# A two-layer graph network on one core: another order for the first loads, another division of the output loop

## The chip, the cores and the metric

The kernel runs on one core of one Trainium2 chip. The metric is the device time of one execution in microseconds. Three runs were made of the kernel before: the median is 2925.94 us.

## The reference, cut to what matters

There are 16 graphs of 1024 nodes with 128 features. `adj` is symmetric in its pattern, not in its values, and about 6% full.

```python
# layer 0: three convolutions on the full adj
h = relu(layernorm(x))
for i in range(3):
    h = h @ W[i] + b[i]
    nh = h / norm(h)                      # per node
    h = (adj * (nh @ nh.T)) @ h           # relu after it, except the last
x = x + h
# layer 1
h = relu(layernorm(x))
adj_d = dilate(adj, mask)                 # rows one after the other drop neighbours, their columns too
h1 = bn(relu(sage(h,  adj_d, Wr1, Wx1, ...)))
h2 = bn(relu(sage(h1, adj_d, Wr2, Wx2, ...)))
h3 = bn(relu(sage(h2, adj_d, Wr3, Wx3, ...)))
return x + (concat(h1, h2, h3) * mf @ Wl + bl) * mf      # mf: the mask as floats
```

`bn` takes its means over all batches and nodes, so nothing of h3's projection can start before the last batch has been through the last `sage`.

## The kernel before, in words

All matrices are float32 and are cut into blocks of 128 x 128; a batch has 8 x 8 of them. The program has four parts.

The **fused first stage** (to about 1720 us) is layer 0 and the dilation together. Both are Python generators. `step0` advances layer 0 by one step, and the loop over `dilation()` advances layer 0 in proportion to estimated costs, so that the two are woven into one program. What an engine then executes is not this order itself: a scheduler sets each engine's instructions in a static order of its own, from priorities and the dependences between tiles. Inside one engine's queue an instruction waits for all that stand before it.

In layer 0 the adjacency of a batch is kept as transposed blocks of one triangle beside the plain blocks of the other. For each block row `q`, taken in the order `SEQ = (0, 7, 1, 6, 2, 5, 3, 4)`, `adj_piece` (L223) loads the block column `nat` through SP's queue (one of two buffers), and `adjT_tile` (L229) loads the plain row (L233), transposes the 8 - q blocks of `nat` on TensorE (L240), copies them out of PSUM on ScalarE into `adjA` (L241) and writes them to DRAM by GpSimd's queue (L242). `adjA` has two places, for an even and an odd batch.

A `Batch` has these steps: `fetch` loads x (L253); `norm` is layer norm and relu, with bn_stats on VectorE (L140) and eight activations on ScalarE (L148); `enter` transposes it to `hT` (L165, L166); `features` multiplies by W (L273) and adds b on VectorE (L277); `turned` makes `nhT`, `scaled` takes the row norms on ScalarE (L299) and makes `hS` on GpSimd (L301). Then for each `q` follow `products` (TensorE L324, VectorE L333 and L336 into `ew`), `turn` (L353, L354), `sums` and `sums_back` (L364, L378).

`layer0` (L419) begins with all eight `adjT_tile` of batch 0, with `enter` and `features` placed among them, then `turned` and `scaled`. Only then come the products. The other batches' pieces are listed in `pieces` with the place (which batch's turn in `order`, which of its eight steps) at which they are to be transposed: batch 1's during the first turn, each later batch's two turns ahead.

Ahead of this the program writes its constants: W and b through ScalarE's queue (L180, L181), the triangular constants `upto`, `off`, `after` from two fills `up` on GpSimd (L188, L190), and the mask: `mi` is loaded through ScalarE's queue (L202), cast on VectorE (L204), transposed on TensorE (L206) and turned into `mf` and `mbias` (L208, L212). `mbias` is first read in the dilation (L586), `mf2 = mf * mf` (L757) in the output loop. The first calls are x of batch 0, two `adj_piece`, `norm`, x of batch 1, and then layer 0's first step (L737 to L742).

In the dilation, each row of adj is loaded by SP (`an`, L545), turned into 0 and 1 on ScalarE (L547, L548), solved by rounds of small matmuls, and scanned on VectorE (L699).

The **first `sage`** (about 1740 to 2180 us) applies the dilated pattern to adj, and the **second and third `sage`** (to about 2870 us) read the result back from DRAM.

The **output loop** (L1067 to L1075) is last. For each batch, `normed` (L1004) makes `hT` with one activation of 128 x 1024 (L1006, two buffers), `project` (L1011) makes two halves of four matmuls into PSUM (L1016, three buffers, shared), and eight VectorE operations (L1072) compute y = pp * mf2 + acc. SP then writes y to `out` (L1075). y lies in pool tag "o", which has two buffers.

Of the kernel before, what the change touches and what calls it, by code (L numbers as in the profile page):

```python
# [8 lines left out]
F32 = mybir.dt.float32  # L9
F16 = mybir.dt.float16  # L10
I32 = mybir.dt.int32
AF = mybir.ActivationFunctionType
ALU = mybir.AluOpType
# [33 lines left out]
def tile_adj_preln_d2(  # L47
# [121 lines left out]
    with ExitStack() as actx:  # L169
# [7 lines left out]
        w0 = pool1.tile([P, 3, P], F32, name="w0")  # L177
        b0 = pool1.tile([P, 3, P], F32, name="b0")
        for i in range(3):
            nc.scalar.dma_start(w0[:, i, :], W[i])  # L180
            nc.scalar.dma_start(b0[:, i, :], bW[i].partition_broadcast(P))  # L181

        upto = pool1.tile([P, P], F16, name="upto")
        off = pool1.tile([P, P], F16, name="off")
        after = pool1.tile([P, P], F16, name="after")
        for fill, value, op in ((0.0, -2.0, ALU.is_ge), (4.0 * FAR, 2.0 * FAR, ALU.is_gt)):
            up = pool2.tile([P, NCH, P], F32, tag="tt", name=f"up_{fill}")[:, 0, :]
            nc.gpsimd.memset(up, value)  # L188

            nc.gpsimd.affine_select(  # L190
                up, up, pattern=[[1, P]], compare_op=op, fill=fill, base=0, channel_multiplier=-1
            )
            if fill:
                nc.vector.tensor_copy(after, up)
            else:
                nc.vector.scalar_tensor_tensor(upto, ident, 2.0 - FAR, up, ALU.mult, ALU.add)
        nc.vector.tensor_scalar(off, ident, -FAR, None, ALU.mult)
        one16 = pool1.tile([P, 1], F16, name="one16")
        nc.vector.memset(one16, 1.0)

        mi = pool2.tile([P, NCH, P], I32, tag="xb", name="mi")[:NB, 0, :]
        nc.scalar.dma_start(mi, nodemask.rearrange("b (c p) -> (b c) p", p=P))  # L202
        mfl = pool2.tile([P, NCH, P], F32, tag="tt", name="mfl")[:NB, 0, :]
        nc.vector.tensor_copy(mfl, mi)  # L204
        mt = ps_sm.tile([P, NB], F32, tag="sm", name="mt")
        nc.tensor.transpose(mt, mfl, ident[:NB, :NB])  # L206
        mf_flat = mf.rearrange("p b c -> p (b c)")
        nc.vector.tensor_copy(mf_flat, mt)  # L208

        mbias = pool1.tile([P, B, NCH], F32, name="mbias")  # L210
        mb_flat = mbias.rearrange("p b c -> p (b c)")
        nc.vector.tensor_scalar(mb_flat, mf_flat, 0.0, NEVER, ALU.is_equal, ALU.mult)  # L212

# [205 lines left out]
        def layer0():  # L419

            pieces = [((0, s), (1, SEQ[s])) for s in range(NCH)]
            for b in range(2, B):
                i = 6 * (b // 2) - 2 + b % 2
                for s in range(NCH):
                    at_ = min(2 * s + 2 - b % 2, 2 * NCH - 1)
                    pieces.append(((i + at_ // NCH, at_ % NCH), (b, SEQ[s])))
            pieces.sort()  # L430
            for s in range(NCH):
                adjT_tile(0, SEQ[s])
                if s < NCH - 2:
                    adj_piece(0, SEQ[s + 2])
                if s == 3:
                    order[0].enter(0)
                    order[0].enter(1)
                if 4 <= s < 4 + NHALF:
                    order[0].features(s - 4)
            order[0].turned()  # L440
            order[0].scaled()
            for (_, _), piece in pieces[:2]:
                adj_piece(*piece)
            yield 0.0
            behind, pieces_at = [], 0
            for i, now in enumerate(order + [None]):
                then = order[i + 1] if i + 1 < len(order) else None
                after = order[i + 2] if i + 2 < len(order) else None
                ended = order[i - 1] if i and order[i - 1] is not then else None
                if now:  # L450
                    now.begin()
                for s in range(NCH if now else LAG):
                    q = SEQ[s]
                    if now:
                        behind.append((now, s, *now.products(s)))
                        yield (NCH - q) * COLS
                    late = None
# [12 lines left out]
                    if not now:  # L470
                        continue
                    while pieces_at < len(pieces) and pieces[pieces_at][0] == (i, s):
                        adjT_tile(*pieces[pieces_at][1])
                        pieces_at += 1
                        if pieces_at + 1 < len(pieces):
                            adj_piece(*pieces[pieces_at + 1][1])
                        yield (NCH - pieces[pieces_at - 1][1][1]) * TURN
                    if ended:
                        if s == 1:
                            ended.fetch()  # L480
                        if s == 3:
                            ended.residual()
                            yield NCH * TURN
                        if s == 5:
                            ended.next_layer()
                    if s == 5 and after and first(i + 2):
                        after.fetch()
                    if then:
                        new = first(i + 1)
                        if s == 0 and new:  # L490
                            then.norm()
                        if s == 3 and new:
                            then.enter(0)
                            then.enter(1)
                            yield NCH * TURN
                        if s == 4 or s == 5:
                            then.features(s - 4)
                            yield CPH * COLS
                        if s == 6:
                            then.turned()  # L500
                            then.scaled()
                            yield NCH * TURN
# [232 lines left out]
            return got is not None  # L735

        batches[0].fetch()  # L737
        adj_piece(0, SEQ[0])
        adj_piece(0, SEQ[1])
        batches[0].norm()  # L740
        batches[1].fetch()
        step0()  # L742
        for weight in dilation():
            done += weight
            while at * total < done * SPREAD * total0 and step0():
# [29 lines left out]
    with ExitStack() as bctx:  # L775
# [289 lines left out]
            ab = batchnorm(l)  # L1065

        for b in range(B):  # L1067
            y = pool2.tile([P, NCH, D], F32, tag="o", name=f"y_{b}")
            for h, pp, a in project(2, b, normed(3, b, ab)):
                for c in range(CPH):  # L1070
                    n = h * CPH + c
                    nc.vector.scalar_tensor_tensor(  # L1072
# [53 lines left out]
```

## Time and profile before

| what | value |
|---|---|
| median of three runs | 2925.94 us (2923.68 to 2931.75) |
| the profiled execution, whole | 2932.24 us |
| its span, first to last instruction | 2930.4 us |
| granted TensorE clock, mean | 0.976 |
| busy: TensorE, VectorE, ScalarE, GpSimd | 2673.3, 1955.9, 1420.2, 452.9 us |
| first transposes of adj (L240) | 17.9 us |
| first products (L324) | 45.63 us |
| first and last y operation (L1072) | 2879.7 and 2925.3 us |

The span is shorter than the time by 1.8 us that lie around it. Times inside the span count from its first instruction. An engine's busy time is a sum over the whole program; which resource decides changes from stage to stage, so stages are read by themselves: busy time by stretch, then who waited for whom, then the chain that is followed back from the last instruction.

### The profile page before, as it was taken

How to read it: one execution, taken by the hardware profiler on the slowest of the kernel's cores; microseconds unless marked ns; L12 is line 12 of the kernel's file. 1: busy time of each engine (PE TensorE's matmuls, PEld its weight loads, DVE VectorE, ACT ScalarE, POOL GpSimd, SP SyncE). 2: the span in 40 equal slices, each digit the busy share in tenths (PEclk: the TensorE clock that was granted, in tenths of full speed). 3: DMA queues.
4: the chain of work that ended last, by engine and by line, in shares of the span. 5: the costliest groups of instructions: out<-in, count | busy, mean ns of one | idle time of the engine just before them, and what ended most of it. 6: DMA issues, size and time to landing. Idle time of an engine off the chain costs nothing.

```text
span 2930.4 us, 51972 instructions
## 1 busy us (share of the span) xinstructions
PE 2673.3 (91%) x18803; PEld 2205.6 (75%) x18803; DVE 1955.9 (67%) x4945; ACT 1420.2 (48%) x4069; POOL 452.9 (15%) x604
## 2 busy tenths in 40 slices
PE   5898998998989989998998979999989999899996
PEld 3666666666666666766666758989979999899996
DVE  2777778877977878788778446777772233455555
ACT  5766667557546546455455323333333333333333
POOL 2111112012011112121112002222220010010010
PEclk9999999999999999999999989999999999999998
DMA  8437258247347456386162039999995666576763
GB/s 268 145 115 219 89 168 247 77 139 229 92 130 219 105 169 188 95 248 176 39 206 105 1 114 403 405 406 404 405 372 173 208 210 202 177 243 222 240 217 115
DMA packets 383017, 585.21 MB, mean 200 GB/s; under 512 B 85201, under 2 KB 267345, under 8 KB 382753
## 3 DMA queue, kind: packets, MB, share of 16 engines
q1 hardware_dynamic: 343280, 425.28, 45.9%
q0 software_dynamic: 38464, 156.07, 14.4%
q8 instruction: 151, 2.47, 0.3%
q14 instruction: 114, 0.93, 0.1%
q10 hardware_dynamic: 1008, 0.46, 0.1%
HBM read 403.44 MB, written 163.58 MB: 193 GB/s over the span
## 4 chain that ended last, share of the span: by engine, by line
PE 56%; DVE 18%; DMA 13%; issue 6%; ACT 4%; POOL 1%; SPq 1%; POOLq 0%; DVEq 0%; another core or an unknown queue 0%; ACTq 0%
PE agg L831 20%; PE po L364 7%; PE pg L324 6%; DVE rank L699 5%; PE pw L803 5%; PE po L378 5%; DVE ew L336 4%; DMA aT<-in_adj_dram 3%; PE gt L353 3%; PE pp L1016 2%; DMA kl<-keep 2%; PE pw L273 2%; DMA an<-in_adj_dram 2%; DMA aT<-adjT 1%; DMA kb<-keep 1%
## 5 line engine op out<-in xcount | busy, mean ns | idle before, releaser
L831 PE MATMUL agg<-hw,aT 128*128 128x128 f32 (+1 forms) x6144 | 742.9, 277 | 8.8 <-DVE aT L941 7.5
L831 PEld LDWEIGHTS agg<-hw,aT 128*128 128x128 f32 x6144 | 712.1, 192 | 14.7 <-DVE aT L941 10.1
L324 PE MATMUL pg<-nhT 128*128 128x512 f32 (+3 forms) x1152 | 457.4, 500 | 71.9 <-DVE ew L336 63.0
L364 PE MATMUL po<-ew,hS 128*128 128x512 f32 (+3 forms) x1152 | 455.3, 499 | 13.8 <-ACT hTo L387 9.9
L336 DVE TENSOR_TENSOR ew<-pg,adjA 128x768 f32<-128x768 f32 (+3 forms) x528 | 425.1, 827 | 4.6 <-DVEq L768 2.7
L378 PE MATMUL po<-ew,hS 128*128 128x128 f32 x2688 | 366.9, 277 | 0.0
L378 PEld LDWEIGHTS po<-ew,hS 128*128 128x128 f32 x2688 | 339.3, 193 | 36.6 <-issue 36.3
L354 ACT ACTIVATE ew<-gt 128x512 f32<-128x512 f32 (+1 forms) x480 | 208.9, 465 | 243.2 <-PE gt L353 240.2
L324 PEld LDWEIGHTS pg<-nhT 128*128 128x128 f32 x1152 | 188.7, 193 | 171.6 <-issue 120.9
L699 DVE TENSOR_TENSOR_SCAN rank<-patt 128x1024 f16<-128x1024 f16 x128 | 294.0, 2307 | 0.9
L364 PEld LDWEIGHTS po<-ew,hS 128*128 128x128 f32 x1152 | 195.8, 194 | 105.6 <-issue 72.9
L353 PEld LDWEIGHTS gt<-ident,ew 128*128 128x128 f32 x1344 | 167.8, 143 | 97.3 <-issue 68.5
L333 DVE TENSOR_TENSOR ew<-pg,adjA 128x128 f32<-128x128 f32 x384 | 108.1, 282 | 196.3 <-PE pg L324 150.9
L353 PE MATMUL gt<-ident,ew 128*128 128x128 f32 x1344 | 212.1, 277 | 4.1 <-ACT ew L354 2.7
L881 POOL TENSOR_TENSOR o<-o,rn 128x512 f32<-128x512 f32 x96 | 107.6, 1121 | 650.4 <-DVE rn L880 646.0
L803 PE MATMUL pw<-wrx,hT 128*128 128x256 f32 x768 | 181.1, 391 | 10.2 <-ACT hT L1006 9.7
L805 DVE TENSOR_TENSOR own<-pw,bs 128x256 f32<-128x256 f32 x192 | 81.4, 424 | 148.0 <-ACT hw L804 148.0
L803 PEld LDWEIGHTS pw<-wrx,hT 128*128 128x128 f32 x768 | 146.3, 196 | 32.7 <-ACT hT L1006 10.5
L959 ACT ACTIVATE aT<-pta 128x512 f32<-128x512 f32 (+3 forms) x160 | 71.2, 466 | 205.0 <-PE pta L958 178.0
L860 DVE SCALAR_TENSOR_TENSOR o<-agg,invdeg,own 128x128 f32<-128x128 f32 x384 | 109.7, 344 | 87.0 <-PE agg L831 78.3
L876 ACT ACTIVATE own<-o 128x128 f32<-128x128 f32 x384 | 114.6, 301 | 103.3 <-DVE o L860 103.2
L301 POOL TENSOR_TENSOR hS<-hN,rn 128x1024 f32<-128x1024 f32 x48 | 94.6, 1970 | 409.2 <-DVE rn L157 300.4
(161 smaller groups left out, 3962.2 us busy)
## 6 DMA issues: line engine op xcount, KB each, us to landing
an<-in_adj_dram SPq DMA_DIRECT2D x128, 512.0 KB, 4.6
keep<-kp POOLq DMA_DIRECT2D x128, 256.0 KB, 3.6
kb<-keep SPq DMA_DIRECT2D x128, 256.0 KB, 5.4
aT<-adT SPq DMA_DIRECT2D x32, 960.0 KB, 5.4
aT<-adT SPq DMA_DIRECT2D x32, 832.0 KB, 5.5
aT<-adT SPq DMA_DIRECT2D x32, 704.0 KB, 4.6
aT<-adT SPq DMA_DIRECT2D x32, 576.0 KB, 3.4
xb<-in_x_dram SPq DMA_DIRECT2D x31, 512.0 KB, 5.1
```

The lines of the kernel that those rows point to most:

```text
L324: nc.tensor.matmul(pg[:, :n, :].rearrange("p c q -> p (c q)"), lhsT=self.nhT[:, q * P : (q + 1) * P], rhs=self.nhT[:, (q + c) * P : (q + c ...
L333: nc.vector.tensor_tensor(ew[:, 0, :], pg[:, 0, :], place[:, 0, :], ALU.mult)
L336: nc.vector.tensor_tensor(both[0][:, :, off, :], pg[:, own:n, :].unsqueeze(1).to_broadcast([P, 2, n - own, P]), both[1][:, :, off, :], ALU ...
L353: nc.tensor.transpose(pt[:, i, :], ew[:, at + i, :], ident)
L354: nc.scalar.activation(ew[:, at : at + n, :], pt[:, :n, :], AF.Copy)
L364: nc.tensor.matmul(self.po[:, c * P : (c + n) * P], lhsT=self.hS[:, q, :], rhs=ew[:, c - q : c - q + n, :].rearrange("p c q -> p (c q)"), ...
L378: nc.tensor.matmul(self.po[:, q * P : (q + 1) * P], lhsT=self.hS[:, q + n, :], rhs=ew[:, NCH - 1 - q + n, :], start=False, stop=closes and ...
L699: nc.vector.tensor_tensor_scan(rank, pt[:, 1 : N + 1], pt[:, 2:], 0.0, ALU.add, ALU.add)
L803: nc.tensor.matmul(pw[:, i, :], lhsT=hT[:, 2 * h + i, :], rhs=wrx[:, l, :], start=True, stop=True)
L831: nc.tensor.matmul(self.place(c), lhsT=aT[:, blk, :], rhs=self.hw[:, source, :], start=source == 0 and c % self.ga == 0, stop=ends(c, source),
L860: nc.vector.scalar_tensor_tensor(self.o[:, c, :], self.place(c)[:, :P], invdeg[:, b, c : c + 1], self.own[:, c, :], ALU.mult, ALU.add,)
L876: nc.scalar.activation(self.own[:, n, :], self.o[:, n, :], AF.Square, accum_out=ss[:, c : c + 1])
```

## The change

At the start, x of batch 0 is requested ahead of adj; W, b and the mask are issued on GpSimd's queue; the mask's work comes after layer 0's first step; the two fills `up` and the mask get small tiles of their own, in place of buffers of the large pool tags "tt" and "xb". Only the first three of batch 0's eight `adjT_tile` are placed ahead of the first products; the other five go into `pieces`, each three steps of the first turn ahead of its own products. At the end, y alternates between the tags "o" and "own", and of the even batches the second half is computed by four activations on ScalarE and one addition on GpSimd.

```diff
         for i in range(3):
-            nc.scalar.dma_start(w0[:, i, :], W[i])
-            nc.scalar.dma_start(b0[:, i, :], bW[i].partition_broadcast(P))
+            nc.gpsimd.dma_start(w0[:, i, :], W[i])
+            nc.gpsimd.dma_start(b0[:, i, :], bW[i].partition_broadcast(P))
...
-            up = pool2.tile([P, NCH, P], F32, tag="tt", name=f"up_{fill}")[:, 0, :]
+            up = pool1.tile([P, P], F32, tag="up", name=f"up_{fill}")
...
-        mi = pool2.tile([P, NCH, P], I32, tag="xb", name="mi")[:NB, 0, :]
-        nc.scalar.dma_start(mi, nodemask.rearrange("b (c p) -> (b c) p", p=P))
...
+            first_few = 3
             pieces = [((0, s), (1, SEQ[s])) for s in range(NCH)]
+            pieces += [((0, s), (0, SEQ[s + first_few])) for s in range(NCH - first_few)]
...
             pieces.sort()
-            for s in range(NCH):
+            ahead = [(0, q) for q in SEQ[:first_few]] + [p for _, p in pieces[:2]]
+            for p in ahead[:2]:
+                adj_piece(*p)
+            order[0].norm()
+            for s in range(first_few):
                 adjT_tile(0, SEQ[s])
-                if s < NCH - 2:
-                    adj_piece(0, SEQ[s + 2])
-                if s == 3:
+                adj_piece(*ahead[s + 2])
+                if s == 1:
                     order[0].enter(0)
                     order[0].enter(1)
-                if 4 <= s < 4 + NHALF:
-                    order[0].features(s - 4)
+            for h in range(NHALF):
+                order[0].features(h)
             order[0].turned()
             order[0].scaled()
-            for (_, _), piece in pieces[:2]:
-                adj_piece(*piece)
             yield 0.0
...
         batches[0].fetch()
-        adj_piece(0, SEQ[0])
-        adj_piece(0, SEQ[1])
-        batches[0].norm()
+        step0()
         batches[1].fetch()
-        step0()
+
+        mi = pool1.tile([P, P], I32, tag="mi", name="mi")[:NB, :]
+        nc.gpsimd.dma_start(mi, nodemask.rearrange("b (c p) -> (b c) p", p=P))
+        mfl = pool1.tile([P, P], F32, tag="up", name="mfl")[:NB, :]
...
         for b in range(B):
-            y = pool2.tile([P, NCH, D], F32, tag="o", name=f"y_{b}")
+            y = pool2.tile([P, NCH, D], F32, tag=("o", "own")[b % 2], name=f"y_{b}")
             for h, pp, a in project(2, b, normed(3, b, ab)):
+                hc = slice(h * CPH, (h + 1) * CPH)
+
+                if b % 2 == 0 and h == 1:
+                    for c in range(CPH):
+                        n = h * CPH + c
+                        nc.scalar.activation(y[:, n, :], pp[:, c, :], AF.Copy, scale=mf2[:, b, n : n + 1])
+                    nc.gpsimd.tensor_tensor(y[:, hc, :], y[:, hc, :], a, ALU.add)
+                    continue
                 for c in range(CPH):
```

More of the change, by code (lines that the diff above doesn't have):

```diff
@@ L199, in tile_adj_preln_d2 @@
         nc.vector.memset(one16, 1.0)
-        mi = pool2.tile([P, NCH, P], I32, tag="xb", name="mi")[:NB, 0, :]
-        nc.scalar.dma_start(mi, nodemask.rearrange("b (c p) -> (b c) p", p=P))
[L203 to L212, printed above, removed]
         adjA = pool1.tile([P, 2, base(NCH), P], F32, name="adjA")
@@ L737, in tile_adj_preln_d2 @@
         batches[0].fetch()
-        adj_piece(0, SEQ[0])
-        adj_piece(0, SEQ[1])
-        batches[0].norm()
+        step0()
         batches[1].fetch()
-        step0()
+        mi = pool1.tile([P, P], I32, tag="mi", name="mi")[:NB, :]
+        nc.gpsimd.dma_start(mi, nodemask.rearrange("b (c p) -> (b c) p", p=P))
+        mfl = pool1.tile([P, P], F32, tag="up", name="mfl")[:NB, :]
+        nc.vector.tensor_copy(mfl, mi)
+        mt = ps_sm.tile([P, NB], F32, tag="sm", name="mt")
+        nc.tensor.transpose(mt, mfl, ident[:NB, :NB])
+        mf_flat = mf.rearrange("p b c -> p (b c)")
+        nc.vector.tensor_copy(mf_flat, mt)
+        mbias = pool1.tile([P, B, NCH], F32, name="mbias")
+        mb_flat = mbias.rearrange("p b c -> p (b c)")
+        nc.vector.tensor_scalar(mb_flat, mf_flat, 0.0, NEVER, ALU.is_equal, ALU.mult)
         for weight in dilation():
```

## The prediction

> **What bounds the kernel now.** I read the stretches of busy time first. The first row below is the head, the next two the time until the fused first stage runs evenly; columns are length, busy time (and instructions) of TensorE, its weight loads, VectorE, ScalarE, GpSimd, then granted clock, DMA share and GB/s.
>
> ```profile
> 0.00:20.00 20.00, 2.38 (x10) 1.97 (x10) 3.75 (x30) 2.31 (x3) 6.97 (x21) 1.00 0.66 182
> 20.00:44.00 24.00, 11.61 (x53) 9.57 (x53) 4.19 (x22) 16.05 (x42) 7.78 (x14) 0.84 0.99 324
> 44.00:68.00 24.00, 20.61 (x107) 13.96 (x106) 10.12 (x33) 19.84 (x44) 4.60 (x6) 0.87 0.94 300
> 68.00:80.00 12.00, 11.07 (x78) 8.29 (x76) 5.38 (x15) 10.81 (x24) 0.51 (x1) 1.00 0.49 164
> ```
>
> For 20 us no engine computes and the DMAs are two thirds used; from 20 to 68 us the DMAs are full (0.99, 0.94); after that they have slack. From 80 to 1740 us TensorE is the bound (about 0.9 busy), so a shift of the head passes through to the end. Why the head is empty stands in the chain of waits and in SP's own waits:
>
> ```profile
> 1.25 4.72 DMA b<-in_L_gnn_b_dram
> 5.98 0.02 issue
> 5.99 10.04 DMA xb<-in_x_dram
> ...
> 18.06 1.74 PE pt_a L240 x9
> 19.80 5.24 DMA nat<-in_adj_dram
> ```
>
> ```profile
> SPq L253 <- DMA b<-in_L_gnn_b_dram: 3.6, 1, 3.6
> ```
>
> x is asked for only at 5.99 us, behind adj and a bias, and lands at 16.0; TensorE's first instruction is the mask's transpose (L206), which waits for VectorE's cast behind x. So transposes start at 17.9 and the first products at 45.63.
>
> The tail is the output loop. In the chain from 2896 us on, the period of two batches is 5.51 us (2900.98, 2906.47, 2911.98), and it is one y buffer's round: eight VectorE operations, then its output DMA, then VectorE again.
>
> ```profile
> 2900.98 2.17 DVE y L1072 x8
> 2903.15 0.02 issue
> 2903.17 3.18 DMA out_dram<-y
> 2906.35 0.03 issue
> 2906.38 0.05 DVEq L1072
> 2906.43 0.04 issue
> 2906.47 2.17 DVE y L1072 x8
> ```
>
> **What the Trainium skill says.** "DMA: Bandwidth & Descriptors", section "Anatomy of one DMA — SWDGE (gpsimd) path", gives a DMA about 2 us fixed and the rest by bytes; for 512 KB that is an estimate of 3.2 us, and the output DMA's median is 3.2 us, so it is nearly alone on the wires and mostly latency: more places hide it. The same page, "Issuing engines are not separate DMA queues", says that another issuing engine saves only issue time; moving W, b and the mask to GpSimd buys no bandwidth, which the trace does not contradict. "ScalarE: Activation LUTs", "What ACT_TABLE_LOAD costs", prices an activation at 186 ns + 0.833 ns an element + 93 ns for each pointer operand; the trace agrees: L148 (128 elements, two pointers) 484 ns against 479, L580 (one pointer, from PSUM) 367 against 386. "SBUF — State Buffer", "SBUF: two separate sides", has VectorE and GpSimd exclude each other when VectorE has two SBUF inputs; L1072 has one in PSUM, so I count no blocking; the trace has no GpSimd work in the tail.
>
> **The change, part by part.**
>
> Tail: places. y alternates between tags "o" and "own", two buffers each, so a batch waits for the output of four batches before: 2.17 + 3.2 us of DMA must fit in two periods, and does. The DMA leaves the chain. Next in line is TensorE and its feeder. Sixteen matmul records take 2.06 us a batch (four stretches of the timeline), 4.12 a pair.
>
> Tail: division. For even batches the second half is four activations and one GpSimd add. VectorE then has 12 operations a pair, 12 x 0.27 = 3.2 us, below 4.12. GpSimd's add of 128x512 is priced by L881, 1.04 us; beside everything. ScalarE has two hT of 1.24 us and four y activations: 1.13 us by L580's rows of four (one pointer each); upper bound 4 x 0.387 = 1.55 by L148's rows (eight in 3.19); lower bound 1.0, four of L354's shortest, 0.25. Sum 3.6 to 4.0 us, also below 4.12. But they form a loop: in ScalarE's queue the four activations of batch e stand ahead of hT for e+2, which TensorE needs for its next pair. TensorE's two halves of e, 2.06; its end to ScalarE, 0.23 (2902.16 + 1.03 to hT at 2903.42); activations 1.13; hT 1.24; to TensorE 0.05. Sum 4.71 us a pair, so 4.7 replaces 5.51 and TensorE idles 0.6 a pair.
>
> Tail: sum. The first pairs run at half clock in both: 24 records in 5.50 us from 2877.55, 1.83 us a half. Walking the four queues with these durations puts the first matmul of batch 4 at 2888.9 and of batches 6, 8, 10, 12, 14 each 4.7 later, at 2912.4; then batches 14 and 15, 4 x 1.03, handover 0.2 and four VectorE operations 1.13: the last y ends at 2917.8 against 2925.6. Gain 7.8; the last two output DMAs, now closer (batch 14's by way of GpSimd), give back some 0.5 us. Tail: 7.3 us; with 1.55 for the activations six loops lose 0.42 each, 4.8. The upper end is 9.
>
> Head: x first. SP issues x at 0.80, where adj's first piece was; that piece, equal in size, landed after 4.9 us, so x lands at 5.7 (bounds: 3.2 by the page's estimate, 10.0 by its own row). Eight bn_stats pairs without strangers between them, 2.43 us (batch 1's, 21.69 to 24.12), root, reciprocal and product 0.85, eight activations 3.19: h is done at 12.2 against 25.8. Then ScalarE copies three adj tiles (1.6), turns a dilation row (1.06, if its DMA has landed; eight transfers, 3.5 MB, are then under way) and copies hT (1.06): 16. A row sum 1.3, the copies of adj tile 1 1.1, matmuls pw 2.1, VectorE's sum, transposes and nhT some 3: first products at about 23.5 instead of 45.6. The table load at 19.57 (1.28 us) moves into the wait for x.
>
> Head: three parts of adj ahead. Nothing is dropped: 20 of batch 0's 36 blocks are transposed after the first products, between batch 1's pieces, as are their DMAs on SP's queue. On TensorE these are 20 x 0.11 = 2.2 us, on ScalarE some 5 us. What decides is DMA: before, 18.6 MB had moved at 68 us (20 x 182 + 24 x 324 + 24 x 300). The same bytes at the mean saturated rate of 312 GB/s from 2 us on end at 61.7, at 324 at 59.4; at 380, the best four microseconds before (32 to 36), at 51. So the 22 us of earlier products shrink to 6 to 17. I take 9: saturation begins at once (eight unblocked issues), but SP then stands at adj part 6 until TensorE has read it, near 13 us.
>
> Head: mask and weights to GpSimd. Seven more issues at its queue's front, 7 x 0.55 = 3.8 us; queued behind are the second `up` fill (VectorE's `after` waits for it, and hN behind that), the first adjT writes, and hS, ahead of which most of the second stage's weights stand at 0.54 us each. W lands by about 7.6 (L759's 6.7 us from 0.9), the mask by some 14 (its 8.9 us after 5); hN is due near 20, hS near 28 and needed near 30: nothing, with that slack of a few us as the cover. The mask's transpose leaves the front of TensorE's queue.
>
> Head: reorder. The order of the instructions of all engines differs locally through the whole fused stage (places shift by tens, with a mean of zero), and is the same from the second stage on. TensorE waits here for VectorE to empty the product banks:
>
> ```profile
> PE pg L324 <- DVE ew L336: 59.9, 47, 3.6
> PE po L364 <- ACT hTo L387: 9.9, 7, 3.5
> PE pc L633 <- DVE E L627: 9.4, 13, 1.6
> ```
>
> All named TensorE waits from 80 to 1740 us are about 140 us. A shuffle that makes a twentieth more or fewer is 7 us either way. I take 0.
>
> Sum: 9 + 7.3 + 0 = 16.3 us, from the profiled execution's 2932.24 (span 2930.4 and 1.8 around it) to about 2916. That execution was 6.3 us above the median of 2925.94; from the median, 2910.
>
> **The rivals.**
> - Head in full: DMA isn't the bound, since before 45 us it moved dilation rows that nobody waited for. Then up to 20 us of head: 2925.9 - 27 = 2899. For: ScalarE and TensorE were 0.83 busy from 44 to 68, so they can use an early start; against: DMA at 0.94 there.
> - Head hidden: what is not transposed before the first products is waited for by products three steps later, and DMA repays nothing. Tail alone: 2919, no change that can be told.
> - The division does nothing: places give the tail its gain and ScalarE's loop takes it (activations at 1.55 us and port blocking); head alone, about 2917.
> - Slower: the shuffled order puts VectorE's `ew` later behind dilation scans (2.3 us each, L699) so TensorE waits at L324. One wait is 59.9 / 47 = 1.27 us; the 16 us gain is eaten by 13 more among 528 such operations, and 20 more make it slower by over 0.3%. At 26 more: 2926 - 16 + 33 = 2943. For: the order was not kept; against: neighbours only trade places and the work is the same.
>
> **How the numbers follow.** Forecast 2902 to 2918, 0.47, at 2910; head in full 0.17; head hidden 0.16; division idle 0.08; slower 0.12. Since about 0.3% (8.8 us) is what a measurement of this kernel can tell from no change, faster means below 2917.2: the forecast nearly whole, the head in full, a little of the next two: 0.72; same 0.18; slower 0.10. The range leaves out the far end of the first rival and most of the slower one: 2896 to 2927.
>
> **What would show it.** Right: first products near 24 us, DMA full from 2 us; the DMAs' slack of 68 us some 9 us earlier; the same lead at the second stage's start (1720 to 1780); output loop with a period near 4.7 us a pair and no wait of y for its output DMA; 38 us from its first VectorE operation to its last instead of 45.9. Wrong: a lead at 60 us that is gone by 1740 (reorder), TensorE's wait at L324 well above 60 us, hS or hN waiting for GpSimd's queue, or a loop that stays at 5.5.

## The result and the profile after

The changed kernel takes 2892.92 us (median of four runs, 2889.37 to 2901.99), the kernel before 2928.85 us on the same chip (four runs, 2923.68 to 2933.79). The ratio is 0.9884, with a 95% interval of 0.9865 to 0.9902. The direction was forecast, and the time lies 17 us below the predicted 2910 and 3 us below the range.

The profiled execution of the kernel after took 2901.99 us (span 2900.3), 9 us above its own median; that of before took 2932.24 (span 2930.4). Their spans differ by 30.1 us. Read at four points of the program, those microseconds come from here:

| stretch | before | after | gain |
|---|---|---|---|
| start to the 73rd product matmul (72 are one batch's) | 150.2 | 146.1 | 4.1 |
| from there to the second stage's first transpose of the pattern (L933) | 1596.1 | 1575.6 | 20.5 |
| from there to the last bn_ab (three `sage`) | 1129.8 | 1133.4 | -3.6 |
| from there to the end: the tail | 54.3 | 45.2 | 9.1 |

Line numbers after are 13 lower from the adj pieces to layer 0's end (L324 is L311), 10 lower in the dilation and 1 higher from the second stage on; the y operations are L1076 (ScalarE), L1077 (GpSimd) and L1081 (VectorE).

**Head.** Busy time by stretch of the kernel after: length, busy time (and instructions) of TensorE, its weight loads, VectorE, ScalarE, GpSimd, then clock, DMA share, GB/s.

```profile
0.00:20.00 20.00, 4.82 (x19) 3.78 (x20) 6.07 (x45) 9.07 (x18) 8.36 (x24) 1.00 0.91 265
20.00:44.00 24.00, 20.89 (x108) 15.29 (x107) 9.16 (x22) 17.63 (x48) 12.65 (x21) 0.93 0.90 283
44.00:68.00 24.00, 18.63 (x112) 13.97 (x110) 6.07 (x28) 17.15 (x37) 1.61 (x3) 0.86 0.97 314
68.00:80.00 12.00, 9.42 (x66) 8.12 (x66) 8.44 (x27) 9.67 (x25) 1.62 (x3) 0.72 0.55 187
```

The DMAs are 0.9 used from the start instead of 0.66, SP's wait of 3.6 us for a bias ahead of x is gone, and x lands 4.2 us after its issue at 0.8:

```profile
L240 SPq DMA_DIRECT2D xb<-in_x_dram x2: 442/979/1516, 0.8 to 4.3; - x2
...
DMA to landing us min/median/max: 4.2/7.7/11.1
```

The first products come at 25.9 us instead of 45.6. Yet one batch's products later the lead is 4.1 us. TensorE's wait for adj in the first 50 us of the kernel after (total us, times, longest):

```profile
PE pt_a L227 <- DMA nat<-in_adj_dram: 15.0, 4, 7.0
```

Before, it was 11.9 us. Most of these 15.0 us lie ahead of the first products; after them TensorE waits only 2.7 us more for adj. So the lead of 20 us is not paid back in waits for adj alone. The rows from the first product to the 73rd, before and after:

```profile
45.63:150.20 104.57, 92.31 (x540) 66.90 (x540) 69.35 (x154) 82.00 (x191) 16.31 (x20) 0.96 0.55 179
25.86:146.10 120.24, 102.69 (x578) 74.95 (x577) 71.10 (x157) 87.59 (x213) 23.47 (x33) 0.90 0.61 198
```

This stretch is 15.7 us longer after. The half clock costs 8.0 us more (12.0 instead of 4.0, half of the time for which the clock records show 0.5), TensorE is idle for 5.3 us more (17.5 instead of 12.3), and the remaining 2.4 us are more work: 38 matmuls, among them the transposes that were put off.

**Fused stage.** The row of the kernel before from the 73rd product matmul to the second stage:

```profile
150.20:1746.30 1596.10, 1449.76 (x9006) 1055.15 (x9006) 1218.86 (x2888) 895.11 (x2411) 242.58 (x310) 0.98 0.49 143
```

And that of the kernel after, between the same points:

```profile
146.10:1721.70 1575.60, 1442.94 (x8989) 1050.56 (x8988) 1208.97 (x2888) 894.90 (x2408) 243.54 (x310) 0.98 0.49 145
```

TensorE's idle time is the length less its busy time: 146.3 us before, 132.7 after. Its busy time falls by 6.8 us, though the work is the same but for some 16 matmuls; 6.8 us is also what the time at half clock cost less (30.7 before, 23.9 after, in the table below). Here the gain arises that the forecast did not contain.

**Tail.** The chain of waits of the kernel after, in its steady part (start, length, what):

```profile
2864.86 1.14 ACT y L1076 x4
2866.00 1.14 ACT hT L1007
2867.13 0.04 issue
2867.18 1.07 PE pp L1017 x8
2868.25 1.06 issue
2869.32 1.14 ACT y L1076 x4
```

The output DMA has left the chain; a pair of batches takes 4.46 us (2864.86 to 2869.32) and its chain is ScalarE's four y activations, hT, and a batch's two halves on TensorE (the 1.06 us called "issue" are the second half).

### The profile page after: what moved, and what is told of

It reads as the page before. It is cut to its first block, busy times and chain, and to the rows that moved or that the text cites. A ratio compares the mean times of both kernels' runs of the same rounds, so it can differ in the third digit from the quotient of the medians.

```text
span 2900.3 us, 52009 instructions
## 1 busy us (share of the span) xinstructions
PE 2667.8 (92%) x18803; PEld 2203.2 (76%) x18803; DVE 1937.8 (67%) x4913; ACT 1426.8 (49%) x4100; POOL 467.5 (16%) x619
## 3 DMA queue, kind: packets, MB, share of 16 engines
q1 hardware_dynamic: 343280, 425.28, 46.4%
## 5 line engine op out<-in xcount | busy, mean ns | idle before, releaser
L311 PE MATMUL pg<-nhT 128*128 128x512 f32 (+3 forms) x1152 | 454.0, 497 | 71.4 <-DVE ew L323 61.3
L311 PEld LDWEIGHTS pg<-nhT 128*128 128x128 f32 x1152 | 188.8, 192 | 174.2 <-issue 131.3
L804 PEld LDWEIGHTS pw<-wrx,hT 128*128 128x128 f32 x768 | 147.0, 197 | 33.5 <-ACT hT L1007 10.5
```

Of the source, the lines that this page charges most:

```text
L311: nc.tensor.matmul(pg[:, :n, :].rearrange("p c q -> p (c q)"), lhsT=self.nhT[:, q * P : (q + 1) * P], rhs=self.nhT[:, (q + c) * P : (q + c ...
L804: nc.tensor.matmul(pw[:, i, :], lhsT=hT[:, 2 * h + i, :], rhs=wrx[:, l, :], start=True, stop=True)
```

## The experiments

All ratios are against runs of the kernel before on the same chip. The experiments ran on four chips, where the kernel before had medians of 2928.52 us (e1 to e4), 2929.40 (e5 to e8), 2926.38 (e9 to e12) and 2923.71 (e13 to e16), so medians of different groups are not compared as they stand. The ratio on record need not be the quotient of the two medians (e2_head: 0.9911 against 0.9933). Idle and lost time are TensorE's, from the 73rd product matmul to the second stage; "lost" is half of the time for which the trace's clock records show 0.5 there. The other times are of the profiled execution; first products, 73rd product and second stage are start times.

| kernel | median us (runs) | ratio to before, 95% | first products | 73rd product | second stage | idle | lost | tail |
|---|---|---|---|---|---|---|---|---|
| before | 2928.85 (4) | | 45.6 | 150.2 | 1746.3 | 146.3 | 30.7 | 54.3 |
| after | 2892.92 (4) | 0.9884, 0.9865-0.9902 | 25.9 | 146.1 | 1721.7 | 132.7 | 23.9 | 45.2 |
| e1_tail | 2915.00 (6) | 0.9939, 0.9923-0.9954 | 45.2 | 147.4 | 1738.8 | 139.6 | 32.4 | 45.3 |
| e2_head | 2908.96 (5) | 0.9911, 0.9892-0.9929 | 26.4 | 143.1 | 1726.2 | 135.5 | 29.0 | 54.1 |
| e3_eight | 2921.20 (16) | 0.9976, 0.9963-0.9988 | 45.1 | 147.8 | 1736.0 | 138.7 | 30.7 | 52.8 |
| e4_late | 2919.23 (6) | 0.9949, 0.9933-0.9964 | 44.0 | 155.6 | 1741.4 | 135.4 | 32.4 | 54.8 |
| e5_same | 2929.16 (22) | 1.0006, 0.9993-1.0018 | 46.6 | 148.2 | 1739.5 | 141.1 | 29.0 | 53.6 |
| e6_places | 2910.28 (6) | 0.9937, 0.9913-0.9962 | 46.7 | 149.6 | 1740.2 | 139.4 | 32.4 | 42.4 |
| e7_divide | 2933.74 (22) | 1.0010, 0.9997-1.0022 | 44.3 | 145.5 | 1734.5 | 139.6 | 27.3 | 57.8 |
| e8_few5 | 2923.24 (22) | 0.9981, 0.9969-0.9993 | 32.8 | 144.8 | 1738.3 | 143.1 | 32.9 | 55.2 |
| e9_no_divide | 2894.44 (6) | 0.9885, 0.9863-0.9906 | 26.9 | 145.1 | 1717.2 | 128.8 | 23.9 | 41.6 |
| e10_first_half | 2891.84 (6) | 0.9874, 0.9851-0.9897 | 27.3 | 145.2 | 1717.7 | 129.9 | 23.9 | 40.5 |
| e11_spread_up | 2921.19 (11) | 0.9976, 0.9959-0.9992 | 46.4 | 149.1 | 1741.8 | 142.2 | 32.4 | 53.9 |
| e12_spread_down | 2916.94 (8) | 0.9957, 0.9941-0.9974 | 49.1 | 151.4 | 1728.1 | 137.2 | 17.1 | 56.3 |
| e13_after_down | 2901.73 (7) | 0.9925, 0.9901-0.9949 | 26.5 | 140.0 | 1723.0 | 137.1 | 23.9 | 40.2 |
| e14_after_up | 2905.25 (6) | 0.9946, 0.9927-0.9965 | 28.2 | 143.5 | 1727.4 | 138.5 | 27.5 | 40.4 |
| e15_two | 2910.28 (20) | 0.9952, 0.9939-0.9964 | 23.6 | 140.4 | 1721.9 | 134.8 | 27.3 | 53.9 |
| e16_four | 2906.15 (11) | 0.9949, 0.9936-0.9962 | 27.7 | 139.4 | 1718.6 | 136.5 | 25.6 | 55.2 |

Runs of one and the same kernel scatter by 3 to 7 us (standard deviation), so single profiles are read for where time goes, and medians and intervals for how much. The expectations set two theories against each other: by the head theory (later: lead theory) the gain comes from the earlier first loads and products, by the order theory from the new static order of the fused stage behind them.

### The two halves of the change

**e1_tail** is the kernel before with the changed output loop, **e2_head** the kernel after with the old one.

```diff
-            y = pool2.tile([P, NCH, D], F32, tag="o", name=f"y_{b}")
+            y = pool2.tile([P, NCH, D], F32, tag=("o", "own")[b % 2], name=f"y_{b}")
...
+                if b % 2 == 0 and h == 1:
...
```

> The kernel before with the new output loop alone (four places for y and the division). Every instruction of the fused stage stands where it stood before. By the traces of the two kernels the stretch after the last batch norm's coefficients took 54.1 us before and 45.1 us in the changed kernel. Order theory (most of the gain comes from the new static order of the fused stage) and head theory (most of it comes from the earlier first loads and products) both expect 9 us, a ratio near 0.997; anything else would mean that the two parts of the change are not independent.

> The changed kernel with the old output loop: head alone. Both theories expect what is left: 21 to 27 us faster, a ratio of 0.991 to 0.993.

The tail alone gives 0.61%, the head alone 0.89%; together 1.50%, against 1.16% (0.98 to 1.35) for the whole change. By the ratios the halves give more than the whole; by the medians they add up, 13.5 + 19.6 = 33.1 us against 35.9. In the profiles the tail is 9 us shorter in e1_tail and unchanged in e2_head, so e1_tail's median falls by more than its tail explains. The head's gain in e2_head lies for the larger part after the 73rd product: the second stage starts 20.1 us earlier, of which 7.1 us were there at the 73rd product (13.0 and 5.0 against the mean of the six profiles with the old order).

### Which part of the head

**e3_eight** has x first and the mask late, but all eight parts of adj ahead, and the old output loop. In the traces the order of TensorE's and VectorE's instructions is that of before from about 130 us to the end of the fused stage; ahead of that it differs in places.

```diff
-            first_few = 3
+            first_few = 8
```

> As e2_head, but all eight parts of batch 0's adj stay ahead of the first products. x is still first, W, b and the mask still go by GpSimd and come later. The order on TensorE and VectorE in the fused stage is then exactly that of the kernel before. Order theory: x lands some 10 us earlier, and of that 3 to 8 us remain at 150 us and still remain at 1640 us; ratio 0.997 to 0.999. Head theory: the early load of x and the unblocked queues are most of the gain, so at least 15 us, a ratio of 0.995 or less.

**e4_late** has the order of the kernel after (in the traces from about 120 us on), but x of batch 0 is loaded four times over, one load after the other; it too has the old output loop.

```diff
-                nc.sync.dma_start(self.xb, x[b].rearrange("(c p) d -> p c d", p=P))
+                for _ in range(4 if b == 0 and self.l == 0 else 1):
+                    nc.sync.dma_start(self.xb, x[b].rearrange("(c p) d -> p c d", p=P))
```

> As e2_head, but x of batch 0 is loaded four times over, each load waiting for the one before, so that it is there some 13 us later. The order on TensorE and VectorE in the fused stage stays that of the changed kernel. Order theory: at 100 to 150 us the lead over the kernel before is near zero or negative, and grows to 10 to 20 us by 1640 us; ratio 0.993 to 0.997. Head theory: without the early x the gain is gone: within 5 us of the kernel before.

**e8_few5** is e2_head with five parts ahead, **e5_same** the kernel before with one more comment.

```diff
-            first_few = 3
+            first_few = 5
```

> The head alone with five parts of adj ahead of the first products instead of three, old output loop. The first products come at about 33 us, and the scheduler finds yet another order for the fused stage. Head theory: the gain lies between three parts (20 us) and eight (7 us), at about 14. Order theory: the lead at 150 us lies between the two, but what follows is anybody's guess: the lead at 1640 us may be anywhere from 0 to 25 us and does not follow the number of parts.

> The kernel before once more with a comment added; every instruction is the same. All theories expect a ratio of 1.000 with its interval across 1. If it is off by 4 us or more, then that much of what the other comparisons show in the fused stage belongs to the single build or to chance and not to the edits: the kernel with the new tail alone was 13 us faster where its tail explains 9.

In e3_eight the first products stay at 45.1 us although x was early: TensorE now waits for adj.

```profile
PE pt_a L227 <- DMA nat<-in_adj_dram: 25.9, 6, 7.4
```

So x first, with W, b and the mask out of the way, brings the first products no earlier by itself; for that it needs fewer parts ahead. The kernel is nevertheless 0.24% (0.12 to 0.37) faster, about 7 us, and its profile does not show where: its 73rd product and its second stage lie within the range of the other profiles with the old order. In e4_late the start is late on purpose:

```profile
PE pt_h L165 <- ACT h L148: 24.5, 1, 24.5
```

Its 73rd product comes 5.4 us later than before's, and still it is 0.5% faster than before. A part of the gain, then, doesn't need the early start at all; with the 5 us that it loses by the 73rd product it makes up some 15 us after it (by the medians), twice e3_eight's 7. In e8_few5 the start is 13 us early (32.8) and the gain is 0.19%, some 6 us, where a gain in step with e2_head's start would be 13. Both point to the order in which the rest of the fused stage is laid out, without showing it yet. e5_same shows no difference, as it should.

### The order by itself

**e11_spread_up** and **e12_spread_down** are the kernel before with another constant for the weave of layer 0 and dilation. Head, tail and work stay; TensorE's and VectorE's order changes all through the fused stage.

```diff
-SPREAD = 0.93
+SPREAD = 0.925
```

> The kernel before with the constant SPREAD at 0.935 in place of 0.93: the weave of layer 0 and dilation, and with it the static order of TensorE and VectorE through the whole fused stage, changes; head, tail and the work stay. Order theory (the static order alone is worth about 10 us in either direction): first products at 45 to 46 us and a tail of 53 to 55 us as before, but the time from the 72nd product group to the last leaves the band of 1561 to 1569 us that six profiles with the old order showed, by 5 us or more, in at least one of the two kernels with a changed SPREAD; the median moves with it. Rival (order is worth nothing, and what moved in the kernel after was the head): both within 1560 to 1570 us and medians within 2925 to 2934.

> The kernel before with the constant SPREAD at 0.925 in place of 0.93, otherwise as the run with 0.935. Order theory: first products and tail as before, the fused stage longer or shorter than 1561 to 1569 us by 5 us or more in at least one of the two. Rival (order is worth nothing): 1560 to 1570 us and a median within 2925 to 2934. A direction is not forecast: nothing in the trace of before tells which order is the better one.

With 0.935 little happens (0.24%); with 0.925 the kernel before gets 0.43% faster, with first products at 49.1 us and a tail of 56.3, both later than before. The fused stage's row of e12_spread_down:

```profile
151.40:1728.10 1576.70, 1439.49 (x9004) 1044.92 (x9001) 1209.64 (x2888) 893.77 (x2411) 241.79 (x310) 0.99 0.49 144
```

1576.7 us, where six profiles with the old order have 1588 to 1596. Idle time is 137.2, and TensorE is 10 us less busy than before with the same work, at a mean clock of 0.99 instead of 0.98. So the order acts in two ways: on how long TensorE waits, and on how often its clock is lowered after a wait. The second can be seen in the timeline of the kernel before; first TensorE's line (in brackets its wait), with 4 matmuls from 1275.31 as the last work ahead of it:

```profile
1277.58 0.55 PE L240 MATMUL pt_a<-ident,nat 128*128 128x128 f32 x3 [1.67 <-DVE hN L283]
```

Then three stretches of 3.4 us, one after the other:

```profile
1275.50:1278.90 3.40, 1.56 (x10) 0.95 (x9) 3.38 (x10) 2.11 (x11) 0.00 (x0) 1.00 1.08 358
1278.90:1282.30 3.40, 3.40 (x11) 2.27 (x11) 2.62 (x9) 2.33 (x5) 0.54 (x1) 0.50 1.04 261
1282.30:1285.70 3.40, 3.40 (x20) 2.38 (x19) 3.40 (x3) 3.32 (x8) 3.19 (x2) 1.00 1.01 333
```

A wait of 1.67 us is followed by 3.4 us at half clock: TensorE is busy throughout and gets 11 matmuls done where the next stretch, of another mix of sizes, has 20. The wait costs some 1.7 us more than its own length.

What decides whether a wait does this comes out when all eighteen traces are read together. Their clock records lie on a fixed grid of 3.41 us. Between the 73rd product and the second stage, a stretch of this grid at full clock in which TensorE was busy for less than 1.4 us was followed by one at half clock in 174 cases of 174, one with more than 2.05 us in none of 7523; of the 330 between, 50 were. Where the grid begins differs from execution to execution (0.6 to 3.4 us after the span's start). So a wait of about 2 us that falls into one stretch lowers the clock, and the same wait cut in two by a grid line need not: a part of the lost time is the luck of one execution. An estimate from the same traces: if their waits are laid on all other starts of the grid, stretches with less than 1.5 us of work number 12 to 18 for the kernel before, 10 to 15 for the kernel after and 6 to 14 for e12_spread_down, whose own execution had 6.

Length less idle time less lost time is 1417 to 1422 us in all eighteen profiles of the table: the work at full clock is the same to 5 us, and these two terms are what differs. (The expectation of e13_after_down says 1421; it was taken with the clock records shifted by 10.6 us against the span.)

**e13_after_down** and **e14_after_up** are the kernel after (the division on the first half, as in e10_first_half below) with the two other values of SPREAD; **e15_two** and **e16_four** are e2_head with two and four parts ahead.

```diff
-SPREAD = 0.93
+SPREAD = 0.925
...
-            first_few = 3
+            first_few = 4
```

> The kernel after with the division on the first half of the even batches, and SPREAD at 0.925. Order theory (the gain beyond the lead of 3 to 7 us belongs to a draw of the static order): the time from the 72nd product group to the second stage's first transpose, 1572.5 us with SPREAD 0.93, moves by 5 us or more in at least one of this run and the next, with first products at 26 to 28 us in both; and in each it equals 1421 us (2 less for the 16 instructions done earlier) + TensorE's idle time + its time lost to the lowered clock, to 3 us. Rival (three parts ahead leave TensorE fewer waits by themselves): 1570 to 1577 us in both. A direction is not forecast.

> As the run before, with SPREAD at 0.935. Order theory: 5 us or more away from 1572.5 us in at least one of the two. Rival: 1570 to 1577 us in both, and medians of 2888 to 2896.

> The head with two parts of adj ahead, the old output loop. Lead theory (the gain grows with the earlier first products): first products near 23 us, and a median of about 2906, 3 us below that with three parts. Order theory: first products near 23 us too, but the fused stage from the 72nd product group on anywhere between 1570 and 1596 us, by its sum 1419 to 1421 us + idle + lost clock; the median follows that, not the first products.

> The head with four parts ahead, the old output loop. Lead theory: first products near 29 us and a median between those with three parts (2909) and with five (2923), about 2914. Order theory: between 1570 and 1596 us from the 72nd product group to the second stage, by the same sum, and a median that may lie above that with five parts or below that with three.

With the same head and another order, 1572.5 us (e10_first_half) become 1583.0 and 1583.9, and the ratio to before goes from 0.9874 to 0.9925 and 0.9946: against these two orders, about 10 us of the kernel after's gain belong to the one that it drew. The row of e13_after_down:

```profile
140.00:1723.00 1583.00, 1445.89 (x8990) 1052.76 (x8989) 1208.82 (x2888) 893.73 (x2408) 243.50 (x310) 0.98 0.48 144
```

That of e10_first_half, to compare it with:

```profile
145.20:1717.70 1572.50, 1442.60 (x8990) 1050.63 (x8988) 1209.27 (x2888) 895.58 (x2408) 243.38 (x310) 0.98 0.49 145
```

The larger part of the difference is TensorE's idle time, 137.1 against 129.9 us. In e13 five of the 10.5 us are offset by an earlier 73rd product (140.0). Against the kernel before on their own chips, two, three and four parts gain 13, 20 and 18 us by the medians (0.48, 0.89 and 0.51% by the ratios), with first products at 23.6, 26.4 and 27.7: the gain does not follow the start, as the lead theory would have it. It need not be a pure draw either: the eight profiles with two to four parts ahead and an early x (1572 to 1584 us, some 2 us of it because 16 matmuls more are done by then) lie below all with the old order (1588 to 1596). Whether fewer parts ahead leave TensorE fewer waits in general, or five parts (1593.4) was the unlucky one, the runs do not settle.

### Which part of the tail

**e6_places** is the kernel before with only the four places (the two lines below), **e7_divide** with only the division.

```diff
-            y = pool2.tile([P, NCH, D], F32, tag="o", name=f"y_{b}")
+            y = pool2.tile([P, NCH, D], F32, tag=("o", "own")[b % 2], name=f"y_{b}")
```

> The kernel before with four places for y and nothing else; VectorE still computes all of y. Places theory: the wait for the output DMA was the whole cost; the loop then runs at VectorE's 2.16 us a batch plus small gaps, some 4.4 to 4.6 us a pair, the same as in the changed kernel (4.46), so 8 to 9 us of tail are gained without the division. Division theory: VectorE and the product banks hold the loop near 5 us a pair and only some 4 us are gained.

> The division alone, with two places for y. Places theory: the way of an even y grows (half product 1.0, four activations 1.1, GpSimd 1.3, DMA 3.2, first half 0.3 and more) to about 6.9 us for two batches against 5.51, so the tail is 8 to 11 us longer than before. Division theory: VectorE's shorter part makes it 2 to 5 us faster.

The places alone bring the tail from 54.3 to 42.4 us, more than the 8 to 9 us expected. The division alone lengthens it to 57.8, 3.5 us instead of the 8 to 11 expected, and the whole is not faster (1.0010). Its waits in the tail:

```profile
DVE y L1080 <- DMA out_dram<-y: 20.8, 14, 2.1
...
PE pp L1016 <- DVE y L1080: 9.4, 8, 1.9
```

With two places y still waits for its output DMA, and TensorE for y; the division only adds two engines to that round.

**e9_no_divide** is the kernel after without the division (the branch below left out), **e10_first_half** with it on the first half of the even batches.

```diff
-                if b % 2 == 0 and h == 1:
+                if b % 2 == 0 and h == 0:
```

> The kernel after, with the four places for y but all y operations left on VectorE. Theory (the places alone make the gain of the tail, and the division gives about 3 us back through ScalarE's loop: the tail was 42.4 us with places alone, 45.2 us with both): the tail from the last bn_ab is 42 to 43 us, and the median lies some 3 us below that of the kernel after, near 2890. Rival (the division is worth something beside the new head, since VectorE has fewer operations per pair): the tail is 45 us or more and the median 2893 or above.

> The kernel after, with the division on the first half of each even batch in place of the second. Theory (what the division costs is order: its four activations stand behind the pair's last product and ahead of the next hT in ScalarE's queue; on the first half they begin one half, about 1 us, sooner, and hT waits no longer): the period of a pair falls from 4.46 us to about 4.1, no wait of TensorE for hT of 0.8 us a pair, tail 42 to 43 us, as without the division. Rival (any ScalarE work in the loop costs its own length, 1.1 us a pair, whichever half it takes): the period stays at 4.4 to 4.5 us and the tail at 45 us.

TensorE's wait for hT in the tail of the kernel after (us in total, times, longest):

```profile
PE pp L1017 <- ACT hT L1007: 9.2, 8, 4.8
```

The same in e10_first_half:

```profile
PE pp L1017 <- ACT hT L1007: 4.8, 1, 4.8
```

On the first half the activations are done while TensorE is at the second; hT waits no longer, seven waits are gone, and the chain of e10_first_half is TensorE alone up to its last batch:

```profile
2854.92 24.85 PE pp L1017 x209
2879.77 0.78 DVE y L1081 x3
```

The tails are 41.6 and 40.5 us against 45.2. The medians, 2894.44 and 2891.84 against 2892.92, can't tell these three kernels apart: 3 to 5 us is the scatter of one run.

## Why the prediction was right and wrong

**x first: right in size, but alone it brings the products no earlier.** x was put at 5.7 us with a lower bound of 3.2; it landed 4.2 us after its issue, at 5.0. (The section that gave the bound describes DMAs issued by GpSimd, and x is issued by SP.) h is done at 11.3 (forecast 12.2), the first products start at 25.9 (23.5).

**Three parts ahead: the direction right, the size too large, the mechanism only in part.** "The 22 us of earlier products shrink to 6 to 17. I take 9": 4.1 us at the 73rd product, and 2 to 5 us in the four kernels with this order and an early x, against the mean of 148.1 for the old order. The lead does shrink, and further than forecast. The bytes give a similar size: by 68 us the kernel after had moved 20 x 265 + 24 x 283 + 24 x 314 = 19.6 MB, before 18.6: 1.0 MB, or 3.2 us at 312 GB/s. I had let the saturated rate begin at 2 us; the first two stretches reached 265 and 283. But that full DMAs are what pays the lead back is not shown: of the 15.7 us, 8.0 are half clock, a cost that the forecast did not have here either, and 2.7 are waits for adj.

**Mask and weights to GpSimd: nothing at the first products, as forecast.** In e3_eight, which has all of that move, the first products come no earlier (45.1 us); why it is 7 us faster in all is open. hS starts at 33.2 instead of the 28 forecast, behind GpSimd's queue, and the first sums follow at 35.6, 10 us after the first products; a cost of this could not be told from that of adj.

**Reorder: the step that failed.** "A shuffle that makes a twentieth more or fewer is 7 us either way. I take 0." In the profiles the fused stage after the 73rd product is 20.5 us shorter: 13.6 of idle time and 6.8 of clock. Taken over several profiles (five with the order of the kernel after, six with the old one), it is 1578 against 1591: 13 us. The zero was not unreasonable as a middle, since the trace names no direction, and SPREAD at 0.935 gave nearly zero (0.24%); the width was wrong. SPREAD alone moved the stage by 14 us on the kernel before and by 10 to 11 us on the kernel after. The width counted waits at their own length and left out that a long one can also halve the clock for 3.4 us. That the draw was a good one was luck: nothing in the forecast pointed to it. Of 146.3 us idle, 79.8 are in 34 waits of 1.5 us or more; after, 65.7 in 26. That is all of the idle time saved. The sign that I had named for it, TensorE's wait for `ew`, pointed the wrong way. Waits of TensorE in the fused stage, before:

```profile
PE pg L324 <- DVE ew L336: 56.2, 45, 3.6
PE po L364 <- ACT hTo L387: 9.9, 7, 3.5
```

And after:

```profile
PE pg L311 <- DVE ew L323: 59.3, 41, 3.6
...
PE po L351 <- ACT hTo L374: 4.3, 6, 1.5
```

The largest sum grew by 3 us while smaller ones went. The other sign named, a lead at 60 us that is gone by 1740, was put for a loss only; the lead grew instead, from 4.1 to 24.6.

**Tail: places undersized, division of the wrong sign.** 7.3 us were forecast, 9.1 measured in the profiles. The loop was right piece by piece: activations 1.14 (1.13), hT 1.14 of the chain (1.24; the activation itself takes 1.25), two halves of 2.13 (2.06); the handover of 0.23 us from TensorE to ScalarE was a few hundredths, so 4.46 us a pair instead of 4.71, and over six pairs that is 1.5 of the missing 1.8 us. But the text took places and division as one gain. Places alone give 11.9; the division, "beside everything" at VectorE's side, takes 3 back through ScalarE's queue. GpSimd's addition takes 1.27 us, not 1.04:

```profile
L1077 POOL TENSOR_TENSOR y<-y,acc 128x512 f32<-128x512 f32 x8 | 10.2, 1270 | 33.5 <-ACT y L1076 30.3 <-issue 3.2
L1076 ACT ACTIVATE y<-pp,mf 128x128 f32<-128x128 f32 x32 | 9.1, 368 | 10.2 <-issue 6.4 <-PE pp L1017 3.8
```

The row that priced it, L881, has one operand that is repeated; this one has three whole tiles. L1076's 368 ns agree with the price in the Trainium skill, "ScalarE: Activation LUTs", section "What ACT_TABLE_LOAD costs" (386 for one pointer, an estimate from that page). VectorE's y operations took 343 ns each before and after, so GpSimd's addition beside them did not slow them, as was counted. No y waits for its output DMA any more, as forecast. From VectorE's first y operation to the start of its last it is 35.6 us (2858.7 to 2894.3), where 38 were forecast.

**The sum.** 9 + 7.3 + 0 in the forecast; 4.1 + 9.1 + 20.5 - 3.6 in the two profiles, where the last is the three `sage`, whose order is the same. These 3.6 us are of the size by which runs of one kernel differ; their cause is open.

**The rivals.** Head in full (2899) is near the time for the wrong reason: the lead at the 73rd product was 4, not 20. Head hidden has the lead at the 73rd product nearly right, but not the whole. Division idle is right in kind: the division takes some 3 us of the places' 12 back, not all of them. The slower case named the right mechanism, the order, and priced it on the bad side; on the good side it was given no case of its own. A case for a better order, priced like the slower one, would have brought 2893 into the range.

**Left open.** The medians of e1_tail and e6_places fall by 14 and 19 us, their profiled tails by 9 and 12. And five profiles with the same order of TensorE and VectorE in the fused stage range from 1572 to 1586 us; the clock explains a part (lost time 23.9 to 32.4 us), and where the grid begins in one execution is a part of that; the rest is not known.

## What to carry to other kernels

Where a static order is laid out by a planner, any edit at its front redraws the order behind it: price that redraw from both sides, by the long waits of the bounding engine and the clock that some of them lower, and give the good side a case of its own. To tell such a draw from what the edit was meant to do, change a constant that only redraws the order, on the kernel before and on the kernel after. When a loop waits for its output buffers, give it buffers first and measure; work moved to another engine must be placed where that engine's next due product doesn't stand behind it.

## What the runs showed of the hardware that was not expected

The clock is lowered after stretches that are only partly idle: with 1.56 us busy between 1275.5 and 1278.9, the following 3.4 us ran at 0.50, and in the eighteen traces less than 1.4 us of work in a stretch was always enough for it. The Trainium skill, "TensorE: Matmul & The Clock Gate", section "Part 1: The HAM clock gate (the "warmup" mystery)", gives half rate after an idle window of about 3.4 us; here the stretches need not be idle throughout, and the measurement decides. That is why the number of long waits alone does not give the number of lowered stretches: e12_spread_down has 26 waits of 1.5 us or more and 6 lowered stretches, the kernel before 34 and 13. The way back asks for more work: of 294 stretches of the grid at half clock, those with more than 2.8 us of work were followed by full clock, those with less than 2.75 by another one at half.

The executions of one kernel follow their clock: over 313 runs of the sixteen kernels of the experiments and the kernel before, each taken against its kernel's mean, 0.001 of mean clock goes with 1.7 us (correlation -0.57). e12_spread_down's eight runs have a mean clock of 0.9818, before's runs on the same chip 0.9797.
